# Layernorm rows through DRAM, 32x32 block transposes on VectorE, and router products on four column parts of the array

## The chip, the cores and the metric

The kernel runs on one core of a Trainium2 chip. The metric is the device time of one execution in microseconds (us). The core's engines work side by side, each through its own list of instructions in order: TensorE (PE, the products; PEld in a profile is its weight load), VectorE (DVE), ScalarE (ACT), GpSimd (POOL) and SyncE (SP), which here only issues DMAs. DMAs issued by SP, ACT and POOL move data between DRAM and the on-chip memory SBUF; products land in PSUM, in eight banks. An engine waits for another, or for a DMA, on semaphores that the program sets.

## The reference

One layer of a transformer on 4 batches of 512 tokens of 512 features, all in float32: a gated linear cross attention against 1024 context rows per batch, then a mixture of 8 experts of which each token uses 2.

```python
def _xattn(query, kv, Wq, Wg, bg, Wkv, Wo):        # 16 heads of 32
    q = query @ Wq.T
    gate = sigmoid(query @ Wg.T + bg)
    k, v = split(kv @ Wkv.T, 2, axis=-1)
    q, k = feature_map(q), feature_map(k)          # x > 0: x + 1, else exp(x)
    kv_summary = einsum('bhsd,bhse->bhde', k, v)
    z = 1 / (einsum('bhld,bhd->bhl', q, k.sum(axis=-2))[..., None] + 1e-6)
    attn = einsum('bhld,bhde->bhle', q, kv_summary) * z
    return attn * gate @ Wo.T

def _ffn(x, Wr, We, be):
    logits = einsum('bsd,de->bse', x, Wr)          # 8 experts
    w, sel = top_k(logits, 2);  w = softmax(w)
    # out = sum over the two chosen experts of w * (x @ We[e] + be[e])

x = x + _xattn(layernorm(x), ctx, ...)
x = x + _ffn(layernorm(x), Wr, We, be)
```

## The kernel before

**Tiles.** 128 partitions carry 128 tokens, or 128 of the 512 features (a chunk, `c`, of which there are `NC` = 4). A batch has `NT` = 4 tiles of tokens and `NS` = 8 tiles of context rows. A product contracts over the partitions, so the tokens have to lie along the columns with the features on the partitions: `xT` is the normalized batch in that form.

**Stages of one batch.** `kv_tiles` runs over the 8 context tiles: four products for the keys `pk` (and their feature map on DVE, ACT and DVE, lines 199 to 201), four for the values `pv`, and four that add the tile before to the summary `kvs`. Every float32 product shows as two passes in the profile. Then `query` makes four groups `pq`, `gate` four groups `pg`, `inverses` the denominators (`pd`, on four column parts of the array), `products` joins them (`pz`, `pn`) and `attention_out` gives `po`, which is added to `x`. The context tiles of the next batch are interleaved: tiles 0 to 3 run between `products` and `attention_out`, tiles 4 to 7 behind it.

**What the change touches.** `layernorm_stats` and `normalize` (lines 207 to 215) make normalized rows. `normalized_T` transposes a tile of them for the attention: four transposes on PE (`transposed`, line 88) and a copy by ACT (line 224). It runs behind each of the context tiles 4 to 7. `choose` does the same for the router with the rows of the batch that has just left the attention: it transposes `row` into `x2T`, multiplies each of the four chunks by the router's weights `wr_sb` with the tokens as the stationary operand and the 8 experts as columns (`pl`), and picks two experts on DVE. It is a generator: a step of it runs behind each of the context tiles, in the last batch behind expert tiles. `dispatch` counts the tokens of every expert (`pp`) and scatters each row into its two experts' streams in DRAM by indirect DMAs of POOL (line 504); it runs between the second and the third query of the next batch.

**Experts.** `listed` makes a list of full tiles on DVE: an early list of 17 after batch 2 and a late list of 22 after batch 3. `run` loads a tile's rows from the stream (`xg`, line 631, on SP, at an address read from the list), transposes them on PE, makes four products `pe`, adds the bias (`y`) and scatters the result (line 669). It loads one tile ahead. Eight stores of a constant tile `empty` fill the rows behind the ends of the streams (line 771) before the late tiles. At the end results are read back, weighted, added and stored.

**Order.** Products and SP's loads are kept in program order (`load`, `matmul`); the rest is ordered by a scheduler that works with its own times. SP's queue carries the context tiles `cT` (three buffers), `x`, the weights, `xg` and the result reads.

Of the kernel before, what the change touches and what calls it, by code (L numbers as in the profile page):

```python
# [9 lines left out]
F32 = mybir.dt.float32  # L10
# [37 lines left out]
def xattn_moe_kernel(  # L48
# [31 lines left out]
    stream = dram.tile([SLOTS + P, ROW], F32, name="stream")  # L80
    result = dram.tile([2 * TOK + LATE * P, F], F32, name="result")


    def matmul(**operands):
        tc.keep_in_program_order(nc.tensor.matmul(**operands))  # L85
# [2 lines left out]
        tc.keep_in_program_order(nc.tensor.transpose(dst, src, ident))  # L88


    def load(dst, src):
        tc.keep_in_program_order(nc.sync.dma_start(out=dst, in_=src))

    def load_ctx(b, s):
        t = cpool.tile([P, ROW], F32, tag="cT", name=f"cT_{b}_{s}")
# [41 lines left out]
    for g, a, b, n in turned:  # L137
        load(wo_sb[b : b + n, g, :], wo[a : a + n, g, :])

# [20 lines left out]
    for g in range(NC):  # L160
        r = slice(g * HD, (g + 1) * HD)
        for i in range(NC):
# [3 lines left out]
                compare_op=ALU.is_equal, fill=0.0, base=-i, channel_multiplier=1,  # L166
            )

    ones = const.tile([P, P], F32, name="ones")
    nc.gpsimd.memset(ones, 1.0)  # L170
    before = const.tile([P, P], F32, name="before")
# [12 lines left out]
        return t  # L184

    home = numbers("home", [[2 * P, B * NT]], [P, B * NT], channel=2)

    empty = const.tile([P, ROW], F32, name="empty")
    nc.gpsimd.memset(empty, 0.0)
    nc.gpsimd.memset(empty[:, D : D + 1], float(2 * SLOTS))  # L190
    unread = numbers("unread", [[P, LATE]], [P, LATE], base=2 * TOK, channel=1)
    expert_no = numbers("expert_no", [[0, GROUPS], [1, E]], [P, GROUPS, E])
    tile_no = numbers("tile_no", [[1, LATE]], [P, LATE])
    steps = numbers("steps", [[0, E], [P, TOK // P]], [P, E, TOK // P])

    def feature_map(dst, src):

        ex = work.tile([P, D], F32, tag="ex", name="ex")
        nc.vector.tensor_scalar(ex, src, 0.0, None, ALU.min)  # L199
        nc.scalar.activation(ex, ex, AF.Exp)  # L200
        nc.vector.scalar_tensor_tensor(dst, src, 0.0, ex, ALU.max, ALU.add)  # L201

    def layernorm_stats(tiles):
        mv = small.tile([P, NT, 2], F32, tag="mv", name="mv")
# [9 lines left out]
    def normalize(dst, xt, t, mv, rstd):  # L214
        nc.vector.tensor_scalar(
            dst, xt, mv[:, t, 0:1], rstd[:, t : t + 1], ALU.subtract, ALU.mult
        )
# [5 lines left out]
            transpose(pt[:, c, :], src[:, ts(c, P)])  # L223
        nc.scalar.copy(dst, pt)  # L224

    def normalized_T(xT, t, tiles, mv, rstd):

        xn = work.tile([P, D], F32, tag="ex", name="xn")
        normalize(xn, tiles[t], t, mv, rstd)
        transposed(xT[:, :, ts(t, P)], xn)  # L230

    def new_xT():
        return big.tile([P, NC, L], F32, tag="xT", name="xT")
# [13 lines left out]

    def keys(b, s):
        k = kvpool.tile([P, D], F32, tag="k", name=f"k_{b}_{s}")
        feature_map(k, half_tile(ctx_tiles[b, s], 0, "pk"))  # L250
        return k

    def values(b, s):
# [24 lines left out]
    sums, pending, made = {}, {}, {}  # L278

    def kv_tiles(b, lo, hi, between=None):  # L280
        for s in range(lo, hi):
            nxt = (b, s + 2) if s + 2 < NS else (b + 1, s + 2 - NS)
            if nxt[0] < B and nxt != (0, 2):
                ctx_tiles[nxt] = load_ctx(*nxt)
            if b in (1, 2) and s % 2 == 0:
                e = (b - 1) * E // 2 + s // 2
                load(we_sb[:, e], we[e])
            if (b, s) == (3, 0):
                load(stream[SLOTS : SLOTS + P, :], empty)
            if s == 0:  # L290
                sums[b] = pkv.tile([P, NC, 2 * P], F32, tag="kvs", name="kvs")
            k = made.pop(s) if s in made else keys(b, s)
            if (b, s) == (0, 0):
                made[1] = keys(0, 1)
            v = values(b, s)
            if s > 0:
                kv_add(sums[b], s - 1, *pending[b])
            pending[b] = k, v
            if between is not None:
                between(s - lo)  # L300
        if hi == NS:
            kv_add(sums[b], NS - 1, *pending[b])

# [113 lines left out]

    def choose(b, mv, rstd):

        pl = pmm.tile([P, NT, E], F32, tag="mm", name="pl")  # L420
        rows, xTs = [], []
# [6 lines left out]
        def logits(t):  # L428
            for c in range(NC):
                matmul(  # L430
                    out=pl[:, t, :],
                    lhsT=xTs[t][:, c, :],
                    rhs=wr_sb[:, c, :],
                    start=(c == 0),
                    stop=(c == NC - 1),
                )
# [24 lines left out]
        m2, hot2, _ = largest("2")  # L461

        routed[b] = rows, m1, hot1, first, m2, hot2
        yield

    def dispatch(b):

# [149 lines left out]
    def run(lists, n, early):  # L617
# [3 lines left out]
        def rows(j):  # L621
# [7 lines left out]
            else:  # L629
                xg = kvpool.tile([P, ROW], F32, tag="v", name="xg", bufs=2)  # L630
            load = nc.sync.dma_start(out=xg, in_=stream[ds(row, P), :])
            if early:
# [6 lines left out]
            xT = work.tile([P, NC, P], F32, tag="qT", name="xgT", bufs=NC)  # L639
            transposed(xT, xg)  # L640
            return xT, xg

        def expert(j, xT, xg):
            no = nc.values_load(
# [34 lines left out]
        ready = rows(0)  # L679
# [8 lines left out]
    ln = layernorm_stats(xs[0])  # L688
    kv_tiles(0, 3, NS, lambda i: i < NT and normalized_T(xT, i, xs[0], *ln))
    kv_blocks(sums[0])  # L690
    for b in range(B):
        more = b + 1 < B
        qTs = [query(g, xT) for g in range(2)]
        if b > 0:
            dispatch(b - 1)
        qTs += [query(g, xT) for g in range(2, NC)]
        aT = big.tile([P, NC, L], F32, tag="aT", name="aT")
        gate(0, xT, aT)
        z = inverses(qTs)
# [19 lines left out]
        products(qTs, z, aT)  # L719
        if more:  # L720
            xs[b + 1] = load_x(b + 1)
            kv_tiles(b + 1, 0, NS // 2)
        else:
            for _ in range(4):
                next(early)
        attention_out(b, aT)
        choice = choose(b, *layernorm_stats(xs[b]))
        if more:
            ln = layernorm_stats(xs[b + 1])
            xT = new_xT()  # L730

            def between(i):
# [4 lines left out]
            next(choice)  # L737
            kv_blocks(sums[b + 1])
    for _ in range(2):
        next(early)  # L740
    for t in range(NT):
        next(choice)
        if t % 2:
            next(early)
    next(choice)
    for _ in range(2):
        next(early)
    dispatch(B - 1)
# [121 lines left out]
```

## Time and profile before

| | |
|---|---|
| Runs before | 649.47, 649.52, 650.05, 650.26 us; median 649.79 |
| The profiled execution | 649.66 us, of it a span of 648.0 from the first to the last instruction |
| Granted TensorE clock, mean | 0.989 |
| A tile of context rows on PE (`pk`, `pv`, `kvs`) | 7.76 us |
| The same with transposes of `xn` and `row` and with `pl` | 9.4 to 9.5 us |
| Four products of 512 columns (eight passes) | 3.43 us |
| One expert tile, with its transposes | 3.87 us |
| DMA over the span | 72.6 MB, 112 GB/s, 28272 packets |

The groups of instructions that the change concerns, by line; the columns are line, engine, operation, tiles, shape, count, busy time and mean of one, then the idle time before it and what ended it:

```profile
L88 PE MATMUL pt<-ident,xn 128*128 128x128 f32 x64 | 9.8, 275 | 2.8 <-DVE xn L215 2.8
L88 PE MATMUL pt<-ident,row 128*128 128x128 f32 x64 | 9.5, 273 | 0.0
L85 PE MATMUL pl<-wr_sb,x2T 128*128 128x8 f32 x128 | 15.4, 247 | 0.2 <-ACT x2T L224 0.2
L224 ACT COPY xT<-pt 128x512 f32<-128x512 f32 x16 | 9.4, 585 | 12.1 <-PE pt L88 12.1
L215 DVE TENSOR_SCALAR xn<-x,mv,rstd 128x512 f32<-128x512 f32 x16 | 8.6, 540 | 0.1
```

Products are pipelined, so the mean of one (275 ns for a transpose) overlaps its neighbours; what one costs is read from the chain, where four transposes take 0.44 us. Idle time of an engine that isn't the bottleneck costs nothing.

### The profile page before, as it was taken

How to read it: one execution, taken by the hardware profiler on the slowest of the kernel's cores; microseconds unless marked ns; L12 is line 12 of the kernel's file. 1: busy time of each engine (PE TensorE's matmuls, PEld its weight loads, DVE VectorE, ACT ScalarE, POOL GpSimd, SP SyncE). 2: the span in 40 equal slices, each digit the busy share in tenths (PEclk: the TensorE clock that was granted, in tenths of full speed). 3: DMA queues.
4: the chain of work that ended last, by engine and by line, in shares of the span. 5: the costliest groups of instructions: out<-in, count | busy, mean ns of one | idle time of the engine just before them, and what ended most of it. 6: DMA issues, size and time to landing. Idle time of an engine off the chain costs nothing. (4 is left out here: it accounts for less than half of the span.)

```text
span 648.0 us, 6400 instructions
## 1 busy us (share of the span) xinstructions
PE 621.4 (96%) x2092; PEld 309.7 (48%) x2092; DVE 238.7 (37%) x565; ACT 137.8 (21%) x219; POOL 116.5 (18%) x256
## 2 busy tenths in 40 slices
PE   7999999999999999999999999999999999999990
PEld 3555543544654344456434545653445644444540
DVE  2222243135145321622542162276333452112564
ACT  1322221113322121233212204222102211111110
POOL 3100000000005000000400000023413375443430
PEclk9999999999999999999999999999999999999995
DMA  8612300220423022022210100034412397449756
GB/s 305 182 33 63 116 0 18 97 81 17 137 108 130 2 97 98 16 81 98 103 44 33 34 0 16 17 153 141 130 49 81 98 299 223 136 156 376 273 193 247
DMA packets 28272, 72.61 MB, mean 112 GB/s; under 512 B 4368, under 2 KB 4368, under 8 KB 26832
## 3 DMA queue, kind: packets, MB, share of 16 engines
q1 hardware_dynamic: 20256, 49.36, 23.2%
q0 software_dynamic: 5680, 18.65, 7.7%
q10 hardware_dynamic: 2304, 4.20, 1.7%
q8 instruction: 17, 0.28, 0.2%
q14 instruction: 15, 0.12, 0.1%
HBM read 46.98 MB, written 25.21 MB: 111 GB/s over the span
## 5 line engine op out<-in xcount | busy, mean ns | idle before, releaser
L85 PE MATMUL pe<-we_sb,xgT 128*128 x312 | 140.3, 594 | 1.1 <-ACT xgT L224 0.5
L85 PE MATMUL pk<-wkv_sb,cT 128*128 128x512 f32 x256 | 118.2, 606 | 4.7 <-DMA wkv_sb<-in_wkv_dram 4.7
L85 PE MATMUL pv<-wkv_sb,cT 128*128 128x512 f32 x256 | 114.9, 592 | 0.0
L85 PEld LDWEIGHTS pe<-we_sb,xgT 128*128 128x128 f32 x312 | 56.5, 191 | 58.6 <-issue 57.6
L85 PEld LDWEIGHTS pv<-wkv_sb,cT 128*128 128x128 f32 x256 | 48.8, 190 | 61.1 <-issue 61.1
L199 DVE TENSOR_SCALAR ex<-pk 128x512 f32<-128x512 f32 x32 | 22.0, 689 | 147.6 <-PE pk L85 147.6
L85 PEld LDWEIGHTS pk<-wkv_sb,cT 128*128 128x128 f32 x256 | 47.6, 194 | 57.8 <-issue 54.0
L256 POOL MEMSET v<- 128x4 f32 x32 | 3.3, 105 | 347.0 <-PE kvs L85 284.0
L658 DVE TENSOR_TENSOR y<-pe,be_sb 128x512 f32<-128x512 f32 x39 | 26.9, 691 | 99.3 <-PE pe L85 87.3
L200 ACT ACTIVATE ex<-ex 128x512 f32<-128x512 f32 x48 | 30.2, 630 | 138.3 <-DVE ex L199 128.4
L85 PE MATMUL pg<-xT,wg_sb 128*128 128x512 f32 x128 | 56.7, 596 | 0.0
L85 PE MATMUL pq<-xT,wq_sb 128*128 128x512 f32 x128 | 56.6, 596 | 0.0
L85 PE MATMUL po<-wo_sb,aT 128*128 128x512 f32 x128 | 55.6, 592 | 0.0
L224 ACT COPY xgT<-pt 128x512 f32<-128x512 f32 x39 | 22.6, 586 | 135.0 <-PE pt L88 120.0
L669 POOL DMA_INDIRECT result<-y,to x39 | 42.1, 1078 | 33.1 <-DVE y L658 24.5
L504 POOL DMA_INDIRECT stream<-row,slot x32 | 32.1, 1002 | 49.6 <-DVE cmp L532 22.5
L85 PEld LDWEIGHTS kvs<-v,k 128*128 128x128 f32 x256 | 33.3, 191 | 13.4 <-issue 13.4
L85 PEld LDWEIGHTS pg<-xT,wg_sb 128*128 128x128 f32 x128 | 24.0, 190 | 32.0 <-issue 32.0
L85 PEld LDWEIGHTS po<-wo_sb,aT 128*128 128x128 f32 x128 | 24.1, 190 | 29.1 <-issue 28.9
L85 PEld LDWEIGHTS pq<-xT,wq_sb 128*128 128x128 f32 x128 | 23.8, 191 | 27.2 <-issue 27.2
L85 PE MATMUL kvs<-v,k 128*128 128x129 f32 x256 | 34.0, 275 | 0.0
L201 DVE SCALAR_TENSOR_TENSOR k<-pk,ex 128x512 f32<-128x512 f32 x32 | 22.1, 691 | 24.1 <-ACT ex L200 24.0
(150 smaller groups left out, 452.9 us busy)
## 6 DMA issues: line engine op xcount, KB each, us to landing
xg<-stream SPq DMA_DIRECT2D x39, 257.0 KB
cT<-in_cT_dram SPq DMA_DIRECT2D x32, 256.0 KB
we_sb<-in_we_dram SPq DMA_DIRECT2D x8, 1024.0 KB
y<-result SPq DMA_DIRECT2D x16, 512.0 KB
x<-in_x_dram SPq DMA_DIRECT2D x16, 256.0 KB
out_dram<-x ACTq DMA_DIRECT2D x16, 256.0 KB
stream<-empty SPq DMA_DIRECT2D x9, 257.0 KB
wkv_sb<-in_wkv_dram SPq DMA_DIRECT2D x8, 256.0 KB
```

Of the source, the lines that this page charges most:

```text
L85: tc.keep_in_program_order(nc.tensor.matmul(**operands))
L199: nc.vector.tensor_scalar(ex, src, 0.0, None, ALU.min)
L200: nc.scalar.activation(ex, ex, AF.Exp)
L201: nc.vector.scalar_tensor_tensor(dst, src, 0.0, ex, ALU.max, ALU.add)
L224: nc.scalar.copy(dst, pt)
L256: nc.gpsimd.memset(v[:, :, P : P + 1], 1.0)
L504: put = nc.gpsimd.indirect_dma_start(out=stream, out_offset=bass.IndirectOffsetOnAxis(ap=slots[i][:, t, :], axis=0), in_=rows[t], in_offse ...
L658: nc.vector.tensor_tensor(y, pe, be_sb[:, ds(no, 1), :].rearrange("p o f -> p (o f)"), ALU.add)
L669: put = nc.gpsimd.indirect_dma_start(out=result, out_offset=bass.IndirectOffsetOnAxis(ap=home_i, axis=0), in_=y, in_offset=None,)
```

## The change

1. Normalized rows no longer go through PE. `normalized_rows` stores a batch's four tiles (`xn`) in a DRAM buffer `normed`; `get_blocks` reads them back with four DMAs, one for each 32 partitions, so that partition `32 i + t` holds, for every group of 32 tokens, token `t` of it and the 128 features of part `i` in runs of 512 bytes; `turn` transposes each 32x32 block on VectorE, which puts features on the partitions. The features then lie in another order than before: `load_rows` brings the weights `wg`, `wq` and the router's in the same order, with four DMAs each in place of one.
2. The same way is taken by the rows of the router: `choose` stores `row`, reads `blocks2` tile by tile (four DMAs for each of four tiles, two tiles at a time since the buffers `z` are two) and turns them into `x2T`.
3. The router's products have the weights stationary, padded to 32 columns, with the tokens as columns; the four chunks go to four column parts of the array (`pr`), without adding up. ACT copies the four partial sums (`routes`), and one product per tile with a folding matrix `fold` of ones adds the parts and turns the result (`pl`).
4. The order: `xn` of the next batch is made and stored behind its second context tile, not behind tiles 4 to 7. `choose` has other steps, and the last of them run between the queries of the next batch. `dispatch` runs behind all four queries. In the last batch two expert tiles, not four, run ahead of `attention_out`, five between the steps of `choose`, two behind it, and eight, not seven, behind `dispatch`.
5. Expert tiles are loaded three ahead, each load ordered behind the latest load of SP. `empty` is no constant any more but is filled twice in a buffer of the pool that the feature map and the lists use (`ex`).

```diff
+    normed = dram.tile([2 * B, L, D], F32, name="normed")
...
-    wr_sb = wpool.tile([P, NC, E], F32, name="wr_sb")
+    router = wpool.tile([P, NC, HD], F32, name="router")
...
+    def load_rows(dst, src):
+        for i in range(NC):
+            load(dst[ts(i, HD)], src.rearrange("(c f) i n -> i f c n", f=HD)[i])
+    nc.gpsimd.memset(router, 0.0)
-    load(wg_in, wg)
+    load_rows(wg_in, wg)
-    load(wq_sb, wq)
-    load(wr_sb, wr)
+    load_rows(wq_sb, wq)
+    load_rows(router[:, :, 0:E], wr)
...
+    def empty_rows():
+        empty = work.tile([P, ROW], F32, tag="ex", name="empty")
+        nc.gpsimd.memset(empty, 0.0)
+        nc.gpsimd.memset(empty[:, D : D + 1], float(2 * SLOTS))
+        return empty
...
+    def put_rows(k, t, rows):
+        load(normed[k, ts(t, P), :], rows)
+    def get_blocks(dst, k, lo, n):
+        for i in range(NC):
+            rows = normed[k, lo * P : (lo + n) * P, ts(i, P)]
+            load(dst[ts(i, HD)], rows.rearrange("(j t) f -> t j f", t=HD))
+    def turn(dst, src):
+        nc.vector.transpose(
+            dst.rearrange("p c (j t) -> p j c t", t=HD),
+            src.rearrange("p j (c f) -> p j c f", f=HD),
+        )
+    def normalized_rows(b, mv, rstd):
+        for t in range(NT):
+            xn = work.tile([P, D], F32, tag="row", name="xn", bufs=NT)
+            normalize(xn, xs[b][t], t, mv, rstd)
+            put_rows(b, t, xn)
+    def normalized_T(xT, b):
+        blocks = big.tile([P, L // HD, P], F32, tag="aT", name="blocks")
+        get_blocks(blocks, b, 0, NT)
+        for t in range(NT):
+            yield
+            turn(xT[:, :, ts(t, P)], blocks[:, ts(t, NC), :])
...
     def choose(b, mv, rstd):
-        pl = pmm.tile([P, NT, E], F32, tag="mm", name="pl")
...
+            put_rows(B + b, t, row[:, 0:D])
...
+        yield
+        pr = pmm.tile([P, L], F32, tag="mm", name="pr")
+        def routed_half(xTs):
+            for t, x2T in xTs.items():
+                for c in range(NC):
+                    matmul(
+                        out=pr[ts(c, HD), ts(t, P)], lhsT=router[:, c, :], rhs=x2T[:, c, :],
+                        start=True, stop=True, tile_position=(0, c * HD),
+                    )
+        xTs = {}
+        for half in range(2):
+            blocks = {}
+            for t in range(2 * half, 2 * half + 2):
+                blocks[t] = work.tile([P, NC, P], F32, tag="z", name="blocks2")
+                get_blocks(blocks[t], B + b, t, 1)
+            yield
+            routed_half(xTs)
+            xTs = {}
+            for t in blocks:
+                xTs[t] = work.tile([P, NC, P], F32, tag="x2T", name="x2T")
+                turn(xTs[t], blocks[t])
+        yield
+        routed_half(xTs)
+        routes = work.tile([P, L], F32, tag="z", name="routes")
+        nc.scalar.copy(routes, pr)
+        yield
+        pl = pmm.tile([P, NT, E], F32, tag="mm", name="pl")
         for t in range(NT):
-            xTs.append(work.tile([P, NC, P], F32, tag="z", name="x2T"))
-            transposed(xTs[t], rows[t])
-            if t > 0:
-                logits(t - 1)
-            yield
-        logits(NT - 1)
+            matmul(out=pl[:, t, :], lhsT=routes[:, ts(t, P)], rhs=fold, start=True, stop=True)
...
+        loaded = [ordered(j) for j in range(min(3, n))]
+        ready = prepared(loaded.pop(0))
         for j in range(n):
-            cur, ready = ready, rows(j + 1) if j + 1 < n else None
+            if j + 3 < n:
+                loaded.append(ordered(j + 3))
+            cur, ready = ready, prepared(loaded.pop(0)) if loaded else None
             expert(j, *cur)
...
-        qTs = [query(g, xT) for g in range(2)]
-        if b > 0:
-            dispatch(b - 1)
-        qTs += [query(g, xT) for g in range(2, NC)]
+        qTs = []
+        for g in range(NC):
+            qTs.append(query(g, xT))
+            if b > 0:
+                next(choice, None)
+        if b > 0:
+            dispatch(b - 1)
...
+            def between(i):
+                if i == 1:
+                    normalized_rows(b + 1, *layernorm_stats(xs[b + 1]))
+            kv_tiles(b + 1, 0, NS // 2, between)
-            kv_tiles(b + 1, 0, NS // 2)
         else:
-            for _ in range(4):
+            for _ in range(2):
                 next(early)
...
             def between(i):
-                normalized_T(xT, i, xs[b + 1], *ln)
-                next(choice)
+                next(choice, None)
+                next(turns, None)
+                if i > 1:
+                    next(turns, None)
...
+    empty = empty_rows()
     for e in range(E):
```

More of the change, by code (lines that the diff above doesn't have):

```diff
@@ L88, in transpose @@
         tc.keep_in_program_order(nc.tensor.transpose(dst, src, ident))
+    latest = {}
     def load(dst, src):
-        tc.keep_in_program_order(nc.sync.dma_start(out=dst, in_=src))
+        latest["load"] = nc.sync.dma_start(out=dst, in_=src)
+        tc.keep_in_program_order(latest["load"])
     def load_ctx(b, s):
@@ L167, in xattn_moe_kernel @@
             )
+    fold = const.tile([P, E], F32, name="fold")
+    nc.gpsimd.memset(fold, 1.0)
+    for g in range(NC):
+        r = slice(g * HD, (g + 1) * HD)
+        nc.gpsimd.affine_select(
+            out=fold[r, :], in_=fold[r, :], pattern=[[-1, E]],
+            compare_op=ALU.is_equal, fill=0.0, base=0, channel_multiplier=1,
+        )
     ones = const.tile([P, P], F32, name="ones")
@@ L186, in xattn_moe_kernel @@
     home = numbers("home", [[2 * P, B * NT]], [P, B * NT], channel=2)
-    empty = const.tile([P, ROW], F32, name="empty")
-    nc.gpsimd.memset(empty, 0.0)
-    nc.gpsimd.memset(empty[:, D : D + 1], float(2 * SLOTS))
     unread = numbers("unread", [[P, LATE]], [P, LATE], base=2 * TOK, channel=1)
@@ L200, in feature_map @@
         nc.scalar.activation(ex, ex, AF.Exp)
-        nc.vector.scalar_tensor_tensor(dst, src, 0.0, ex, ALU.max, ALU.add)
+        return nc.vector.scalar_tensor_tensor(dst, src, 0.0, ex, ALU.max, ALU.add)
     def layernorm_stats(tiles):
@@ L224, in transposed @@
         nc.scalar.copy(dst, pt)
[L226 to L230, printed above, removed]
+    def put_rows(k, t, rows):
[20 more added lines that the diff above has]
+            turn(xT[:, :, ts(t, P)], blocks[:, ts(t, NC), :])
     def new_xT():
@@ L249, in keys @@
         k = kvpool.tile([P, D], F32, tag="k", name=f"k_{b}_{s}")
-        feature_map(k, half_tile(ctx_tiles[b, s], 0, "pk"))
+        mapped[s] = feature_map(k, half_tile(ctx_tiles[b, s], 0, "pk"))
         return k
@@ L276, in kv_blocks @@
             nc.vector.tensor_copy(h_ks[r, :, h : h + 1], psum[r, :, P : P + 1])
-    sums, pending, made = {}, {}, {}
+    sums, pending, made, mapped = {}, {}, {}, {}
     def kv_tiles(b, lo, hi, between=None):
@@ L288, in kv_tiles @@
             if (b, s) == (3, 0):
-                load(stream[SLOTS : SLOTS + P, :], empty)
+                load(stream[SLOTS : SLOTS + P, :], empty_rows())
             if s == 0:
@@ L299, in kv_tiles @@
             if between is not None:
-                between(s - lo)
+                with tc.issue_after(mapped[s].ins):
+                    between(s - lo)
         if hi == NS:
@@ L418, in choose @@
     def choose(b, mv, rstd):
-        pl = pmm.tile([P, NT, E], F32, tag="mm", name="pl")
-        rows, xTs = [], []
+        rows = []
         for t in range(NT):
@@ L424, in choose @@
             normalize(row[:, 0:D], xs[b][t], t, mv, rstd)
+            put_rows(B + b, t, row[:, 0:D])
             nc.gpsimd.tensor_copy(row[:, D : D + 1], home[:, b * NT + t : b * NT + t + 1])
             rows.append(row)
[L428 to L436, printed above, removed]
-        for t in range(NT):
-            xTs.append(work.tile([P, NC, P], F32, tag="z", name="x2T"))
-            transposed(xTs[t], rows[t])
-            if t > 0:
-                logits(t - 1)
-            yield
-        logits(NT - 1)
+        yield
[4 more added lines that the diff above has]
+                    matmul(
+                        out=pr[ts(c, HD), ts(t, P)],
+                        lhsT=router[:, c, :],
+                        rhs=x2T[:, c, :],
+                        start=True,
+                        stop=True,
+                        tile_position=(0, c * HD),
+                    )
+        xTs = {}
[16 more added lines that the diff above has]
+        pl = pmm.tile([P, NT, E], F32, tag="mm", name="pl")
+        for t in range(NT):
+            matmul(out=pl[:, t, :], lhsT=routes[:, ts(t, P)], rhs=fold, start=True, stop=True)
         lg = small.tile([P, NT, E], F32, tag="lg", name="lg")
@@ L463, in choose @@
         routed[b] = rows, m1, hot1, first, m2, hot2
-        yield
     def dispatch(b):
@@ L631, in rows @@
             load = nc.sync.dma_start(out=xg, in_=stream[ds(row, P), :])
+            latest["load"] = load
             if early:
@@ L638, in rows @@
                 behind(load, written["stream"], "tokens of the tile")
-            xT = work.tile([P, NC, P], F32, tag="qT", name="xgT", bufs=NC)
-            transposed(xT, xg)
-            return xT, xg
+            return xg
         def expert(j, xT, xg):
@@ L677, in expert, with prepared, ordered @@
                 tc.declare_no_dep(put.ins, got.ins, reason="no token of these is in the tile")
-        ready = rows(0)
+        def prepared(xg):
+            xT = work.tile([P, NC, P], F32, tag="qT", name="xgT", bufs=NC)
+            transposed(xT, xg)
+            return xT, xg
+        def ordered(j):
+            with tc.issue_after(latest["load"].ins):
+                return rows(j)
+        loaded = [ordered(j) for j in range(min(3, n))]
+        ready = prepared(loaded.pop(0))
         for j in range(n):
-            cur, ready = ready, rows(j + 1) if j + 1 < n else None
+            if j + 3 < n:
+                loaded.append(ordered(j + 3))
+            cur, ready = ready, prepared(loaded.pop(0)) if loaded else None
             expert(j, *cur)
@@ L687, in xattn_moe_kernel @@
     kv_tiles(0, 0, 3)
-    ln = layernorm_stats(xs[0])
-    kv_tiles(0, 3, NS, lambda i: i < NT and normalized_T(xT, i, xs[0], *ln))
+    normalized_rows(0, *layernorm_stats(xs[0]))
+    turns = normalized_T(xT, 0)
+    kv_tiles(0, 3, NS, lambda i: next(turns, None))
     kv_blocks(sums[0])
@@ L692, in xattn_moe_kernel @@
         more = b + 1 < B
-        qTs = [query(g, xT) for g in range(2)]
+        qTs = []
+        for g in range(NC):
+            qTs.append(query(g, xT))
+            if b > 0:
+                next(choice, None)
         if b > 0:
             dispatch(b - 1)
-        qTs += [query(g, xT) for g in range(2, NC)]
         aT = big.tile([P, NC, L], F32, tag="aT", name="aT")
@@ L728, in xattn_moe_kernel @@
         if more:
-            ln = layernorm_stats(xs[b + 1])
             xT = new_xT()
+            turns = normalized_T(xT, b + 1)
             def between(i):
-                normalized_T(xT, i, xs[b + 1], *ln)
-                next(choice)
+                next(choice, None)
+                next(turns, None)
+                if i > 1:
+                    next(turns, None)
             kv_tiles(b + 1, NS // 2, NS, between)
-            next(choice)
             kv_blocks(sums[b + 1])
-    for _ in range(2):
+    for _ in choice:
         next(early)
[L741 to L745, printed above, removed]
     for _ in range(2):
```

## The prediction

> **What bounds the kernel now.** I read the page's first part, then what TensorE (PE) waited for, then the chain that ended last between 380 and 460 us, then DVE, SP and POOL in order of time around 440 us.
>
> ```profile
> span 648.0 us, 6400 instructions
> PE 621.4 (96%) x2092; PEld 309.7 (48%) x2092; DVE 238.7 (37%) x565; ACT 137.8 (21%) x219; POOL 116.5 (18%) x256
> ```
>
> ```profile
> engine line waited for: us in total, times, longest us
> PE pk L85 <- DMA wkv_sb<-in_wkv_dram: 4.7, 1, 4.7
> PE pt L88 <- DVE xn L215: 2.8, 3, 0.9
> PE pe L85 <- ACT xgT L224: 0.5, 2, 0.3
> ```
>
> PE is the bound and hardly waits. Of the span's 26.6 idle us, 4.7 stand at the start and about 21 behind the last product at 626.7. So a product taken away shortens the kernel by its own time, and a new wait of PE lengthens it by its own.
>
> ```profile
> 401.07 0.87 PE pt L88 x8
> 401.95 0.79 PE pl L85 x8
> 402.74 3.54 PE pk L85 x8
> ...
> 423.58 6.97 PE pq L85 x16
> ...
> 441.52 1.00 PE pd L85 x8
> ```
>
> The columns are start, length and what ran. A context tile of batches 1 to 3 carries eight transposes (four of `xn`, four of `row`) in 0.87 us and the router's four products (eight passes) in 0.79 us.
>
> ```profile
> 448.43 0.12 DVE L614 CAST rowiA<-rowA 128x17 int32<-128x17 f32 x1
> 449.57 48.77 SPq L631 DMA_DIRECT2D xg<-stream  x13
> 452.43 0.39 POOL L664 TENSOR_SCALAR at<-xg,rankedA 128x1 f32<-128x1 f32 x1 [9.20 <-DMA xg<-stream]
> 457.09 1.09 PE L88 MATMUL pt<-ident,xg 128*128 128x128 f32 x8
> ```
>
> Here the reader sees the latency of a load: issued at 449.57, landed by 452.43, so 2.9 us; PE uses it at 457.09, so 4.7 us are to spare. From the list's last number to the issue goes 1.0 us.
>
> **What is removed.** Transposes of `xn` and `row`: 2 x 16 tiles x 0.44 = 14.0 us. Router products: 16 x 0.79 = 12.6 us. The three waits for `xn` go with the transposes behind them: 2.8 us. Together -29.4 us, all on PE. ACT loses 32 copies of 0.59, which bound nothing.
>
> **What is added on PE.** The router runs 4 products of 32 columns per tile, each on its own quarter of the array, over 128 tokens. The nearest row is `pd`: eight passes over 512 tokens on four quarters in 1.00 us, where eight full passes of `pg` take 3.43; a quarter of that is 0.86, so 0.14 is overhead. For 128 tokens this gives 0.86/4 + 0.14 = 0.35 us per tile. The other bound is 0.79, what eight passes with loads cost in `pl`. I take 0.40, near `pd`, since the array is parted the same way: 6.4 us (5.6 to 12.6). The folding product has `pl`'s form, 0.79 per batch: 3.2 us. Sum so far -19.8.
>
> **The turn on VectorE.** No row shows a 32x32 transpose. The nearest are 128x512 SBUF operations: `xn` at 0.54 and the matmul-side ones at 0.69; bounds 0.54 to 1.3 (twice the latter would be two passes), taken 0.6. 32 of them are 19 us on an engine that is 37% busy, so only their place counts. In the built order of batches 0 to 1 and 1 to 2, DVE runs: exponent input of the first `pq`, turn of tile 2, `qT`, turn of tile 3; PE has the router's second half directly behind that first `pq`. From the end of `pq`: 0.2 + 0.69, turn 0.6, `qT` 0.69, turn 0.6, release 0.2 = 3.0 us, against 0.4 of product meanwhile: 2.6 us of stall, twice, 5.2. In batch 2 to 3 the turns stand ahead of the exponent: nothing. In the last batch turn 1 stands behind `y` of the fifth expert tile and turn 3 behind `y` of the sixth: each 0.2 + 0.69 + 0.6 + 0.1 less 0.4 = 1.2 us, 2.4.
>
> [...]
>
> **The detour through DRAM.** SP gets 112 more DMAs (16 stores of `xn`, 16 of `row`, 16 reads of `blocks`, 64 of `blocks2`) and 9 more in the prologue; four `x` loads took 1.85 us, so 0.46 us each. In the built program a DMA on SP also waits until the eighth before it has landed. I follow one transition from the end of `po`. `row` is normalized from 6.9 to 9.1 us (later than before by the exponent of the fifth tile); four stores are issued 7.6 to 9.2; four `blocks` reads of 256 KB 9.6 to 11.0; `cT_7` at 11.5; eight `blocks2` reads behind it. PE needs `cT_7` at 23.3 (three tiles of 7.76) and `xT` only at 32. `blocks` reads move 512-byte rows, 32 per DMA engine and read. The profile's queue part bounds a row: q1 took 119 ns per packet of 2.4 KB (23.2% of 16 x 648 us over 20256 packets), so 25 ns by bytes and 119 by count. At 60, between them, a read takes 1.9 us and `cT_7` lands at 11.6 + 4 x 1.9 + 0.8 = 20.0: hidden, 3.3 to spare. At 119 it lands at 27.6: 4.3 late, three times.
>
> **Waits that are moved.** `xn` of the next batch is now made in the second context tile: statistics and normalizing in one burst, 4 x (0.68 + 0.18 + 0.54) = 5.6 us on VectorE, which makes the third tile's `k` about 2 us later; PE adds it only after another tile of 7.76: nothing, and 0 to 1 without that tile. POOL's start gets a fill and four selects, under 1.5 us while PE waits 4.7 for weights: nothing.
> Prologue: nine more issues ahead of `cT_3` on SP. Before it went out at 23.32, needed at 29.43; 4.1 us later plus 2.9 of landing is 30.3, and `wg`, `wq` in 32-partition parts won't land earlier: 1.5 us (0 to 4).
> `dispatch` goes from behind two queries to behind four, 6.97 us later. In batch 3 the early list then ends behind the 3.35 us reciprocal: `rowiA` some 15.6 us after `pp`, load out at 16.6, landed at 19.5, against 18.9 for PE: 1.0 us with the second load (0 to 3).
> Last batch: `xg` number 5 stands on SP behind the four stores of `row`, which wait for VectorE: rows ready 3.7 to 5.3 us after `po`, load out at 6.8, landed at 9.7, needed at 7.75 after two tiles: 1.9 us (0 to 3).
> Late list: `empty` was a constant; now it is filled on POOL behind the list and, in the built order, behind the eight scatters and a result scatter. From `pp`: scatters to 12.7, then 1.3, 0.9, 0.5, 1.4, 0.8: 17.7; eight fills at 1.21 each (9.65 in the trace) to 27; landed 29.3; load out 29.5, landed 32.4. PE has eight expert tiles to cover it, 30.6 us: 2.0 us (0 to 6). Behind SP here wait the late loads, and PE for them.
> Loading three expert tiles ahead in place of one gains nothing: PE waits 0.5 us for them in all.
>
> **Sum.** -29.4 + 6.4 + 3.2 + 5.2 + 2.4 + 1.5 + 1.0 + 1.9 + 2.0 = -5.8 us. The profiled execution took 649.66 (span 648.0 and 1.66 around it), the median of the runs is 649.79: 649.8 - 5.8 = 644.0. The terms' bounds hardly fall on one side together, so I add them as squares. Upwards: products 0.55 a tile +2.4 (0.79 is a rival below), six turns of 1.3 +4.2, prologue +2.5, first list +2.0, `xg` +1.1, late list +4.0: 7.1. Downwards: products -0.8, last batch's turns -2.4, prologue -1.5, -1.0, -1.9, -2.0: 4.2. This case alone: 640 to 651.
>
> **Rivals.**
> Reads bind (slower). One mechanism: four `blocks` reads ahead of `cT_7` and of the turns. It decides from 85 ns per 512-byte row, where 11.6 + 4 x 2.7 + 0.8 reaches 23.3. At q1's 119 ns: 3 x 4.3 = 12.9 us, 649.8 - 5.8 + 12.9 = 656.9. For it: 32 partitions a read and four times the packets per byte; against it: outgoing queue q10 took 76 ns a packet of 1.8 KB, below the point. 22%.
> [...]
> Quarters don't run side by side, so the change doesn't do what it says: 0.79 per tile, 12.6 in place of 6.4: 650.2. For it: passes are short here, 128 columns against the 512 of `pd`. 15%.
> Waits absorbed: DVE and SP run ahead of what I laid out, and only products count: 649.8 - 19.8 = 630.0, with prologue 631.5. For it: DVE has 63% idle; against it: its order is fixed, and the turn does stand behind `pq`. 13%.
>
> **Chances.** The forecast has 50%, the rivals 22, 15 and 13. A run can be told from no change at 0.2%, 1.3 us: 648.5 to 651.1 is the same. Faster: 0.44 of the forecast's, 0.13, 0.02 of the quarters' case: 0.59. Same: 0.03 and 0.05: 0.08. Slower: 0.03, 0.08 and 0.22: 0.33. The range takes in both outer cases: 631 to 657.
>
> **What would show it.** No `pt<-ident,xn` or `row`; `pr` near 0.4 us a tile; PE waiting for the turn 2.6 us behind the first `pq` of batches 1 and 2; PE waiting for `xg` once near `po` of batch 3 and once at the first late tile; `pk` never waiting for `cT` beyond the prologue. PE waits for `cT_7`, or turns that wait on `blocks`, would show the first rival; `pr` at 0.8 the second. A busy sum of PE below 600 with no waits above 10 us in all would make the prediction wrong on the fast side.

## The result, and the profile after

The changed kernel takes 650.1 us (median of 42 executions, 647.9 to 654.5), the kernel before 649.6 (median of 64, 648.4 to 650.7): a ratio of 1.001 with a 95% interval of 1.0003 to 1.0017. So nothing that matters came of the 5.8 us that were forecast. Two things are to be seen at once: the median hardly moved, and the executions spread over 6.6 us where those of before spread over 2.3.

The first part of the page of the kernel after, and what PE waited for (engine, line, what it waited for, then us in all, times, longest):

```profile
span 649.7 us, 6450 instructions
...
PE 611.6 (94%) x1996; PEld 290.4 (45%) x1996; DVE 259.6 (40%) x597; ACT 123.0 (19%) x191; POOL 118.7 (18%) x264
```

```profile
PE pr L87 <- DVE x2T L264: 7.1, 6, 1.4
...
PE pk L87 <- DMA cT<-in_cT_dram: 4.3, 1, 4.3
PE pt L90 <- DMA xg<-stream: 3.7, 3, 2.8
```

PE's busy time fell by 9.8 us (621.4 before) and its idle time rose by 11.5 (649.7 - 611.6 = 38.1, against 26.6). The prediction had -17.0 for the products and -2.8 + 14.0 = +11.2 for the waits. As a sum the waits are right to 0.3 us, which is partly luck: the term for the start is 2.8 too low, most others are too high; the products are 7.2 us short. Yet each new product costs about what was taken for it. The groups of the new operations, columns as before:

```profile
L264 DVE STREAM_TRANSPOSE x2T<-blocks 128x512 f32<-128x512 f32 x16 | 11.0, 690 | 5.0 <-DMA blocks<-normed 3.5 <-PE pr L87 1.4
L87 PE MATMUL pr<-x2T,router 128*32 128x128 f32 x128 | 6.0, 282 | 7.1 <-DVE x2T L264 7.1
```

A turn takes 0.69 us, and the chain of waits gives 0.42 us for the router's eight passes of a tile. What is missing shows in the same chain (start, length, what ran), in the transition from batch 0 to 1:

```profile
192.29 0.71 DVE x2T L264
193.00 0.04 issue
193.04 0.42 PE pr L87 x8
193.47 5.33 PE pq L87 x8
198.79 0.79 PE pl L87 x8
```

Four products of 512 columns took 3.43 to 3.54 us in the kernel before, behind its first context tile; this `pq` takes 5.33. The stretches around it, with start and end, length, busy time of PE, PEld, DVE, ACT and POOL, then the granted clock, the DMA share and GB/s, show why:

```profile
154.00:187.00 33.00, 33.00 (x122) 17.19 (x121) 12.71 (x22) 6.64 (x11) 0.80 (x5) 1.00 0.53 144
187.00:193.00 6.00, 3.62 (x16) 1.30 (x14) 3.27 (x8) 1.45 (x5) 0.01 (x1) 1.00 0.99 326
193.00:196.00 3.00, 2.96 (x12) 1.34 (x13) 0.00 (x0) 0.58 (x1) 0.00 (x0) 0.63 0.55 227
196.00:199.00 3.00, 3.00 (x10) 1.41 (x9) 0.17 (x1) 0.00 (x0) 0.00 (x0) 0.80 0.00 0
```

PE is full until 187 at clock 1.00, waits for 2.4 us in two pieces (1.40 and 1.02, one tile of `pr` between them), and then runs for some 4 us at a lower clock, while VectorE, ScalarE and the DMA engines do less than in the 6 us ahead. The same stands behind three other waits of this execution: `pk` behind `cT_3` takes 6.74 us (+3.3), `pq` of the next transition 5.33 (+1.9), and behind the wait of 2.8 us for `xg` four transposes take 1.09 and `pe` 4.67 (+0.65 and +1.2). The first and the last of them in order of time on PE (start, length, what ran, in brackets the wait), and the stretch of that `pk`, columns as before:

```profile
34.03 6.74 PE L87 MATMUL pk<-wkv_sb,cT 128*128 128x512 f32 x8 [4.30 <-DMA cT<-in_cT_dram]
...
487.64 1.09 PE L90 MATMUL pt<-ident,xg 128*128 128x128 f32 x4 [2.78 <-DMA xg<-stream]
488.72 4.66 PE L87 MATMUL pe<-we_sb,xgT 128*128 x8
```

```profile
34.00:38.00 4.00, 3.97 (x5) 1.85 (x6) 0.00 (x0) 0.00 (x0) 0.00 (x0) 0.50 0.76 292
```

Together 3.3 + 1.9 + 1.9 + 1.9 = 9.0 us of slow products that the prediction had at nothing.

### The profile page after: what moved, and what is told of

It reads as the page before. It is cut to its first block, busy times and chain, and to the rows that moved or that the text cites. A ratio compares the mean times of both kernels' runs of the same rounds, so it can differ in the third digit from the quotient of the medians.

```text
span 649.7 us, 6450 instructions
## 1 busy us (share of the span) xinstructions
PE 611.6 (94%) x1996; PEld 290.4 (45%) x1996; DVE 259.6 (40%) x597; ACT 123.0 (19%) x191; POOL 118.7 (18%) x264
## 4 chain that ended last, share of the span: by engine, by line
PE 84%; DMA 5%; DVE 4%; SPq 3%; issue 2%; POOL 1%; ACT 1%; DVEq 0%; POOLq 0%; ACTq 0%
PE pk L87 18%; PE pv L87 16%; PE pe L87 15%; PE pg L87 9%; PE po L87 8%; PE pq L87 8%; PE kvs L87 4%; PE pt L90 2%; PE pz L87 1%; SPq L96 1%; PE pn L87 1%; DVE x L886 1%; DMA cT<-in_cT_dram 1%; DMA xg<-stream 1%; DMA y<-result 1%
## 5 line engine op out<-in xcount | busy, mean ns | idle before, releaser
L87 PE MATMUL pk<-wkv_sb,cT 128*128 128x512 f32 x256 | 120.8, 617 | 9.1 <-DMA wkv_sb<-in_wkv_dram 4.8
L87 PE MATMUL pq<-xT,wq_sb 128*128 128x512 f32 x128 | 60.5, 626 | 0.0
```

## The experiments

The theory: a wait of PE costs itself and a stretch of lowered clock behind it. Each run is set against the kernel before on the same chip (its median was 648.8 to 650.0 there). The last column is the ratio to it with its 95% interval. Where a run is set against the kernel after (650.1 us, beside a kernel before of 649.6), up to 0.8 us of the difference can be the chip's.

| Run | Median us | Ratio |
|---|---|---|
| loads of router and `wo` later | 643.7 | 0.9918 (0.9903 to 0.9932) |
| router's last steps later | 646.9 | 0.9970 (0.9958 to 0.9982) |
| products that fill the waits | 645.1 | 0.9948 (0.9934 to 0.9962) |
| first two together | 639.1 | 0.9862 (0.9843 to 0.9880) |
| turns ordered first | 642.2 | 0.9897 (0.9883 to 0.9911) |
| four tiles ahead | 648.1 | 0.9984 (0.9967 to 1.0001) |
| best | 631.0 | 0.9720 (0.9703 to 0.9737) |
| only `xn` by DRAM | 650.7 | 1.0011 (1.0002 to 1.0021) |
| only the router changed | 640.8 | 0.9856 (0.9838 to 0.9873) |
| only `xn`, loads later | 643.0 | 0.9906 (0.9892 to 0.9920) |
| only the router, repaired | 638.5 | 0.9839 (0.9819 to 0.9859) |

**The start.** The loads of `router` and `wo` go behind the third context tile:

```diff
-    load_rows(router[:, :, 0:E], wr)
-    for g, a, b, n in turned:
-        load(wo_sb[b : b + n, g, :], wo[a : a + n, g, :])
...
     kv_tiles(0, 0, 3)
+    load_rows(router[:, :, 0:E], wr)
+    for g, a, b, n in turned:
+        load(wo_sb[b : b + n, g, :], wo[a : a + n, g, :])
```

> The loads of the router and of wo leave SP's queue ahead of cT_3 and go out behind the third context tile. Theory (a PE wait costs itself and a stretch of lowered clock behind it): the wait of 4.2 us for cT_3 goes, and the pk behind it takes 3.4 us, not 6.74: 650.1 - 4.2 - 3.3 = 642.6 us. Rival A (the slow pk comes from something else in that stretch, such as the copies of wg on POOL or the DMA traffic): only the wait goes, pk stays near 6.7: 645.9. Rival B (the loads that are moved make a later load late): a wait for cT or wo appears, 646 to 650.

643.7 us, 1.1 above the theory's number and 2.2 below that of rival A, 645.9. With 0.8 us for the chip the time alone wouldn't decide between them; the profile does: PE no longer waits for `cT_3`, and its `pk` takes 3.70 us in the timeline in place of 6.74.

**The router later.** `choose` goes on behind the second and third query, `dispatch` behind the first gate product:

```diff
-            if b > 0:
+            if b > 0 and g > 0:
                 next(choice, None)
-        if b > 0:
-            dispatch(b - 1)
         ...
         gate(0, xT, aT)
+        if b > 0:
+            dispatch(b - 1)
```

> The router's last two steps run one query later, and dispatch behind the first gate product. Theory: the waits for the turn behind the first pq of batches 1 and 2 (about 2.0 us each) go, and with them the slow pq behind each (5.33 in place of 3.43): 650.1 - 2 x (2.0 + 1.9) = 642.3 us, less up to 1 us for the later dispatch before the early list. Rival A (the slow pq isn't caused by the wait): only the waits go, 646.1. Rival B (VectorE is the limit there, the wait only moves one query on): 649 to 650.

646.9 us, a miss by 4.6. Part of rival B is true: VectorE's order was made anew, the turn of tile 3 stands behind the next feature map, and PE waits 1.05 us in each transition in place of 2.4. The clock stays up there: in the first transition the `pq` behind the wait takes 3.70 us in the timeline. But the early list comes later, and the profile has two new waits of 0.7 and 0.5 us at its first tiles. With the 1.05 us that is left twice this makes 3.3 of the 4.6; the rest stays open.

**The waits filled.** The run that tells a wait from what follows it:

```diff
+    def busy(n):
+        ps = pmm.tile([P, D], F32, tag="mm", name="busy")
+        for _ in range(n):
+            matmul(out=ps, lhsT=ident, rhs=wkv_sb[:, 0, 0:D], start=True, stop=True)
     def keys(b, s):
+        if (b, s) == (0, 3):
+            busy(4)
...
             for t, x2T in xTs.items():
+                if b < 2 and t > 1:
+                    busy(1)
```

> Products whose result nobody reads fill the waits of PE: four (3.4 us) ahead of the pk that waits for cT_3, one (0.86 us) ahead of the router's products of tile 2 and one ahead of tile 3 in batches 0 and 1. Nothing is ready earlier than before. Theory (the clock falls because PE stands still): the waits shrink by what fills them and end at the same time, the clock stays near 1, pk takes 3.4 and both pq 3.4 us: 650.1 - 3.3 - 2 x 1.9 = 643.0 us. Rival (traffic or turns in that stretch slow PE, or the profile's rows are modelled so): no gain, 650 to 652, and pk and pq as slow as before.

In the profiled execution `pk` starts at 34.03 us, as in the kernel after, and takes 3.70 in place of 6.74; the `pq` behind the turns takes 3.70 in the timeline in place of 5.40. The same two stretches, first in the kernel after, then in this run, 3.0 us earlier, columns as before:

```profile
190.04:193.34 3.30, 0.88 (x17) 0.32 (x16) 2.62 (x4) 0.63 (x1) 0.00 (x0) 1.00 1.02 392
193.40:197.10 3.70, 3.70 (x9) 1.64 (x6) 0.00 (x0) 0.58 (x1) 0.00 (x0) 0.55 0.34 140
```

```profile
187.00:190.30 3.30, 2.76 (x21) 0.80 (x19) 2.62 (x4) 0.63 (x1) 0.00 (x0) 1.00 1.03 391
190.30:194.00 3.70, 3.70 (x18) 1.73 (x10) 0.00 (x0) 0.59 (x1) 0.00 (x0) 1.00 0.34 140
```

The DMA engines are as busy as in the kernel after (0.34, 140 GB/s) and the turns as late, and the clock is 1.00 in place of 0.55. Span against span it is 642.7 to 649.7, 7.0 us where 7.1 were expected, and 6.4 of it stand at the three places. The medians differ by 5.0 only (the profiled execution of the kernel after took 651.6 us, its median is 650.1), 2.1 short of the forecast. More work on PE made the kernel faster: the low clock is due to PE standing still, not to traffic or to VectorE.

**Both.** The first two edits together:

> The edits of the two runs before together: the loads of the router and wo behind the third context tile, the router's last steps one query later. Theory: both savings add, 650.1 - 7.5 - 7.8 = 634.8 us, faster than the kernel before by 15 us. Rival (only waits count, without a clock behind them): 641.9. Rival (waits come back elsewhere): 645 to 650.

639.1 us: 11.0 below the kernel after, more than either rival allows, and 4.3 short of the theory, about the second edit's miss.

**The order on VectorE.** Only an order of instructions is added; the built order swaps the turns and the first query's feature map in batches 1 and 2:

```diff
-        nc.vector.transpose(
+        return nc.vector.transpose(
...
-                turn(xTs[t], blocks[t])
+                latest["x2T"] = turn(xTs[t], blocks[t])
...
-            qTs.append(query(g, xT))
+            if b > 0:
+                with tc.issue_after(latest["x2T"].ins):
+                    qTs.append(query(g, xT))
+            else:
+                qTs.append(query(g, xT))
```

> On VectorE both turns of the router's second half stand ahead of the first query's feature map, nothing else is changed. Theory (the order on VectorE makes the turns late): PE no longer waits behind the first pq of batches 1 and 2, and that pq's successor takes 3.4 us: 650.1 - 2 x (2.0 + 1.9) = 642.3 us. Rival (the reads of blocks2 for tile 3 land only after pq has ended, since they stand on SP behind the two buffers z): VectorE now waits with the feature map behind it, PE still waits, 649 to 652.

642.2 us, the theory's 642.3. In VectorE's queue of the kernel after, turns and feature map alternate, the second turn issued behind `qT` (start, length):

```profile
190.23 0.69 DVE L224 TENSOR_SCALAR ex<-pq 128x512 f32<-128x512 f32 x1 [1.53 <-PE pq L87]
190.84 0.70 DVE L264 STREAM_TRANSPOSE x2T<-blocks 128x512 f32<-128x512 f32 x1
191.68 0.69 DVE L226 SCALAR_TENSOR_TENSOR qT<-pq,ex 128x512 f32<-128x512 f32 x1
192.29 0.70 DVE L264 STREAM_TRANSPOSE x2T<-blocks 128x512 f32<-128x512 f32 x1
```

VectorE had been idle for 1.53 us before. With the order swapped both turns run in that idle time, from 1.5 to 0.2 us ahead of the feature map's first operation: the blocks were there, the order was late.

**Four tiles ahead.** `run` loads tile `j + 4`, not `j + 3`, and four at first:

> Expert tiles are loaded four ahead, not three, so the load of the sixth tile is issued ahead of the stores of row in the last batch. Theory: the wait of 2.3 to 3.0 us for xg behind po goes, and in the executions in which the clock fell behind it 1.2 to 1.9 us more: 650.1 - 2.8 - 1 = 646.3 us (645.4 to 647.5). Rival (PE's wait has another cause, or SP now waits for the fifth buffer and holds up the stores of row): 649 to 651.

648.1 us (644.2 to 651.8). The interval reaches 1, and the 2.0 us below the kernel after are small beside its spread of 6.6: inconclusive as a time. In its profile the wait for `xg` behind `po` is gone (1.0 us left of 3.7), as expected, but another turn of the last batch now makes PE wait, for 1.5 us; the waits for turns there are 2.8 us in all, in place of 2.3.

**Waits of known length.** The kernel before, with a small product, a chain of ScalarE copies and a product of the result ahead of every second context tile; the chain grows with each:

```diff
+    def gap(n):
+        ps = pmm.tile([P, P], F32, tag="mm", name="ahead_of_gap")
+        matmul(out=ps, lhsT=ident, rhs=ident, start=True, stop=True)
+        nc.scalar.copy(held_back, ps)
+        for _ in range(n):
+            nc.scalar.copy(held_back, held_back)
+        ps = pmm.tile([P, P], F32, tag="mm", name="behind_gap")
+        matmul(out=ps, lhsT=ident, rhs=held_back, start=True, stop=True)
     def keys(b, s):
+        if s % 2 == 1 and (b, s) != (0, 1):
+            gap(2 * ((b * NS + s) // 2))
```

> The kernel before, with fifteen waits of PE of growing length (0.6 to about 8 us, a chain of ScalarE copies between two small products) ahead of every second context tile; no transfer and no other work of the stage is changed. Theory (the clock falls after PE has stood still, by chance between about 2 and 4 us): pk and pv behind a wait under 1.6 us take 6.9 us, behind one of over 4 us about 3.3 us more, in between either. Rival (a wait alone does nothing to the clock): 6.9 us behind all of them, and the time is longer by the waits only.

769.7 us in one execution. Four of the fifteen waits, in order of time on PE (start, length, what ran, in brackets the wait):

```profile
30.21 0.49 PE L85 MATMUL behind_gap<-held_back,ident 128*128 128x128 f32 x2 [1.01 <-ACT held_back L255]
30.53 3.60 PE L85 MATMUL pk<-wkv_sb,cT 128*128 128x512 f32 x8
...
49.25 0.49 PE L85 MATMUL behind_gap<-held_back,ident 128*128 128x128 f32 x2 [1.94 <-ACT held_back L255]
49.58 3.60 PE L85 MATMUL pk<-wkv_sb,cT 128*128 128x512 f32 x8
...
68.95 0.49 PE L85 MATMUL behind_gap<-held_back,ident 128*128 128x128 f32 x2 [2.60 <-ACT held_back L255]
69.28 5.29 PE L85 MATMUL pk<-wkv_sb,cT 128*128 128x512 f32 x8
...
428.37 0.79 PE L85 MATMUL behind_gap<-held_back,ident 128*128 128x128 f32 x2 [8.58 <-ACT held_back L255]
428.95 4.85 PE L85 MATMUL pk<-wkv_sb,cT 128*128 128x512 f32 x8
```

Behind 1.01 and 1.94 us `pk` is at its 3.60 (modelled ends overlap, in the chain 3.43); behind all thirteen waits of 2.60 to 10.24 us it is not: 4.85 to 6.06, on average 1.70 more, and from 3.7 us on the small product takes 0.3 more too. A longer wait doesn't cost more, so the expected +3.3 behind a long wait was too much; sizes near it, 3.1 to 3.3, were seen behind `cT_3` only (the kernel after, the second run and that with four tiles ahead).

**The best.** The edits of the first run, of the order (in the last batch also ahead of the expert tile's bias) and of four tiles ahead:

> Four edits together: the loads of the router and wo behind the third context tile, both turns ahead of the feature map on VectorE (in the last batch also ahead of the expert tile's bias), expert tiles loaded four ahead. Theory: -6.4 for the loads as measured, -7.8 for the turns, -3.8 for xg, -2.5 for the last batch's turns from 650.1: 629.6 us. Rival (as in the two runs of parts in this set: turns that wait for their blocks, xg that waits elsewhere): 638 to 644.

631.0 us, 1.4 above the theory's number and faster than both kernels. The first part of its page, and its waits:

```profile
span 629.2 us, 6451 instructions
...
PE 602.5 (96%) x1996; PEld 287.1 (46%) x1996; DVE 260.0 (41%) x597; ACT 122.9 (20%) x191; POOL 118.7 (19%) x264
```

```profile
PE pk L87 <- DMA wkv_sb<-in_wkv_dram: 4.5, 1, 4.5
PE pr L87 <- DVE x2T L261: 2.2, 2, 1.9
PE pt L90 <- DMA xg<-stream: 1.0, 2, 0.6
...
```

PE runs the same 1996 products as in the kernel after, in 602.5 us in place of 611.6: 9.1 us less, near the 9.0 of slow products counted above (0.6 of it is `pr`, 5.4 in place of 6.0). Its idle time is 26.7 us, as in the kernel before (26.6).

**The parts alone.** First the router undone, then the way of `xn`, each as in the kernel before (the functions `choose` and `normalized_T` and their loads of weights are taken over from it):

> The router alone goes back: row is transposed on TensorE and pl made with the tokens stationary, as in the kernel before; xn still goes through DRAM. From 650.1 us: transposes 16 x 0.44 = +7.0, pl 16 x 0.79 = +12.6, pr 16 x 0.43 and the folding 4 x 0.79 away, -10.1: +9.5 of products. Theory (what the router's way saves it gives back in waits for turns, 7.1 us, in the clock behind them, 3.8, in the late load of xg, 2.8 + 1.2, and in the router's three more loads ahead of cT_3, 1.5): 650.1 + 9.5 - 16.4 = 643.2 us, so the router's part alone is a loss. Rival (the router's part gains and the loss lies in the detour of xn): 655 to 660.

650.7 us, a miss by 7.4. The turns' waits go as expected, but `cT_3` is still 5.5 us late (not 2.7), with 2.5 of slow `pk`, and in the last batch PE waits 3.0 us for `row`, which is now needed sooner.

> The attention's rows alone go back: xn is transposed on TensorE behind context tiles 4 to 7, wg and wq come in one load each; the router keeps its way through DRAM. From 650.1 us: transposes 16 x 0.44 = +7.0 and the waits for xn +2.8; SP has six loads fewer ahead of cT_3, 2.8 us, so its wait falls from 4.2 to 1.4 and the clock stays up, -6.1. Theory: 653.7 us; the turns behind the first pq stay late by 2.4 us, with the slow pq behind them. Rival (the reads of blocks, which come first on SP, are what makes the router's turns late): these waits go too, -8.6, 645.

640.8 us, a miss by 13, on the rival's side and 4 below it: PE doesn't wait for `xn` either, where 2.8 us were expected. The turns of the second half stand ahead of the feature map without being told to, PE waits for none of them outside the last batch, and for `cT_3` 0.2 us. Among these runs the order of VectorE that makes the turns late arises only where `xT` has turns too. Not shown is by which of its steps the scheduler came to it.

> The run with the old router (only xn goes through DRAM, 650.65 us), with the loads of the router and wo moved behind the third context tile. Theory (what the detour of xn saves was eaten at the start: 5.5 us of waiting for cT_3 and 2.4 of slow pk behind it, since wg and wq come in parts of 32 partitions): 650.65 - 7.9 = 642.8 us. Rival (the detour loses its gain in the steady stages, in row, xg or the turns): 648 or more.

643.0 us: as the theory has it (by the ratios to the kernel before, 1.0011 and 0.9906, the gain is 6.8 us). The detour's loss lay at the start.

> The run with the old way of xn (only the router is changed, 640.8 us), with the turns ordered ahead of the feature map and four expert tiles loaded ahead. Against the best run (631.0), which differs in the detour of xn. Theory (once its waits are gone the detour is worth its 16 transposed tiles, 16 x 0.44 = 7.0 us): 638.0 us. Rival (the detour is worth nothing even then): 631 or less.

638.5 us. Against the best run, the detour of `xn` is worth 7.5 us once its waits are gone (7.0 expected).

## Why the prediction was wrong

The step that failed stands in its first part: "a new wait of PE lengthens it by its own". It also lowers the clock of what follows. Every wait was priced without that, and 9.0 us of slow products took the gain. The busy time of the best run makes the account of the profiled executions: products -18.9 (602.5 - 621.4), slow products +9.0, waits +11.5, sum +1.6; the spans differ by +1.7. That the median, 650.1, falls on the number of the quarters' rival, 650.2, is chance: its mechanism isn't there.

- Idle time before: the prediction puts the end of the last product at 626.7 and 21 us behind it. It ends at 630.2, with 17.8 behind it; the rest of the 26.6 are the waits that it lists. The sum doesn't rest on this.
- Products: -17.0 predicted, -18.9 shown by the best run. `pr` 0.40 taken, 0.42 measured behind a wait and 0.64 for two tiles in a row, where eight passes of a quarter of 512 columns one behind another would be 3.43 / 4 = 0.86 a tile: the quarters run side by side, and that rival falls. `pr` is 5.4 us in all in the best run, 1.0 less than taken; the other 0.9 isn't broken down.
- Turns behind the first `pq`: 2.6 predicted, 2.4 measured, twice, by the mechanism given, which the run with the order swapped shows. Last batch 2.4 predicted, 7.1 - 4.8 = 2.3 measured. A turn 0.6 taken, 0.69 measured.
- Start: 1.5 predicted, 4.3 measured, and 3.3 of slow `pk`. The step counted issues on SP (4.1 us) and only named the parts of 32 partitions, without a price for them. `cT_3` went out at 29.77, 6.45 later than before, and landed 4.2 us later, not 2.9. With `wg` and `wq` in one load each the wait is 0.2.
- First early list 1.0 predicted, none measured; `xg` behind `po` 1.9 predicted, 2.8 measured; late list 2.0 and 0.9: together 4.9 and 3.7.
- Reads bind: fell. PE waited for no `cT` beyond the start. The four reads of `blocks` ran at 213 to 227 GB/s; 1.05 MB at 222 are 4.7 us for 128 rows of an engine, 37 ns a row, below the 60 taken and the 85 from which it decides.
- Waits absorbed: fell for the kernel after. Its 630.0 is what the best run nearly reaches (631.0), once the waits are taken away.

The two parts aren't independent. Alone, on one chip, the router's is worth 9.2 us (640.8 against 650.0) and the detour's costs 0.7; with the waits repaired both together are worth 17.9 (630.96 against 648.83, on another chip).

## What to carry to other kernels

Price a new wait of TensorE by two numbers, its length and the slow products behind it: here 1.2 to 3.3 us, in some executions from a length of about 2.1 us on and in all from 3.3, and nothing below 2 unless two waits stand close together. A kernel that is bound by PE and hardly waits has more to lose by a few waits than the sum of them shows (here 11.5 us of waits and 9.0 of slow products), so read the granted clock behind each wait, not its mean. An order of instructions that a scheduler chose on another engine is a thing to look at, and an order swapped there was worth 7 to 8 us.

## What the hardware showed

**The clock.** For a single wait, whether it falls is settled by the length up to about 2 us (never behind 1.0 to 1.9) and from 3.3 us on (always, in the run of known lengths and for `cT_3` in five profiles; in four of them the clock is 0.50 to 0.62 from 34 to 38 us). In between the length doesn't settle it, and it looks like chance: in the last batch it fell behind 2.14, 2.31, 2.78, 2.88, 3.00 and 3.02 us, and did not behind 2.17, 2.26 and 3.01 in other runs (3.00 and 3.01 are the same wait for `row` in two of them). Waits of 1.40 and 1.02 with 0.42 of work between them brought it down in all six transitions profiled (the kernel after, the first run and that with four tiles ahead): the `pq` behind them takes 5.1 to 5.4 us. Other pairs differ: 1.03 and 0.92 in the last run did not, nor did 0.27 and 1.94 in the best. The kernels also start with slow products: in eleven profiles the first 16 passes of `pk`, behind the first wait of 4.3 to 4.8 us, take 8.73 to 9.85 us where 16 passes of `pv` take 7.03. The clock shown there is 1.00 (kernel before, 4.60 to 9.00 us), so that these are due to the clock is not shown.

The spread of the kernel after goes with the clock: over the 42 executions its mean clock lies between 0.972 and 0.982, and the time falls by 5.2 us for each 0.01 of it (correlation -0.82; median 651.2 us at 0.975, 648.4 at 0.981), while the kernel before has 0.988 to 0.990.

Why the clock falls from these lengths on, no run shows.

**Loads into 32 partitions.** In the kernel before, mostly `x`, then mostly `wg`, each in all 128 partitions (start and end, length, busy times, clock, DMA share, GB/s):

```profile
12.00:13.50 1.50, 1.50 (x5) 0.58 (x4) 0.69 (x1) 0.04 (x1) 0.00 (x0) 1.00 1.10 407
13.50:15.00 1.50, 1.50 (x5) 0.75 (x4) 0.89 (x2) 0.16 (x1) 0.00 (x0) 1.00 1.04 419
```

In the kernel after, `wg` in four parts of 32:

```profile
14.00:15.50 1.50, 1.50 (x5) 0.73 (x4) 1.25 (x2) 0.53 (x1) 0.00 (x0) 1.00 1.07 205
```

The DMA engines are shown as equally busy and move half. The size of a packet isn't the reason: `x` before and `wg` after both move in packets of 2 KB (0.61 MB in 309 packets from 12.00 to 13.50, 32 of them under 512 bytes, and 0.31 MB in 168 from 14.00 to 15.50, 18 under 512 bytes), `wg` before mostly in 8 KB (69 of 113 packets from 13.50 to 15.00 have that size or more). What holds a load into 32 partitions back, no run shows. At the start it goes with a late `cT_3`: with `wg` and `wq` in one load each PE waited 0.2 us for it, with both in parts of 32 partitions 3.9 to 5.5, unless loads ahead of it were moved or products filled the wait. The difference holds SP's issues too: 2.68 and 1.75 us for the four parts of `wg` and `wq` in the kernel after, 0.33 and 0.35 with one load each.
